# Seven-product projections at the border of layers 0 and 2, and PSUM rings kept by hand

## The chip, the core and the metric

The kernel runs on one core of one Trainium2 chip. The metric is the device time of one launch in microseconds (us), lower is better; three runs of the kernel before gave 2554.56 to 2558.83 us with a median of 2555.19 us.

## What is computed

Four images of 512 channels and 32 x 32 = 1024 positions (tokens), all in float32, pass through four residual layers. Cut to what matters:

```python
# layer 0: attention of 8 heads; scores mixed across heads, softmax, then an instance norm over each head's map
x = x + L0(_gn(x))
    q, k, v = w_q @ x, w_k @ x, w_v @ x            # 512x512 by 512x1024 each
    attn = softmax(einsum('gh,bhqT->bgqT', w_head, q k^T * scale))
    attn = (attn - mean) / sqrt(var + EPS) * in_gamma + in_beta
    out = (attn v).reshape(b, t, c) @ w_proj.T + b_proj
# layer 1: a gate per channel from the means of the channels
x = x + L1(_gn(x))
# layer 2: plain attention of 8 heads
x = x + L2(_gn(x))
    q = Wq @ x + bq;  k, v = split(Wkv @ x + bkv)
    out = Wp @ (softmax(q k^T * SCALE) v) + bp
# layer 3: 2048 memory rows of 512; the best 8 of each token, weighted by a softmax
x = x + L3(_gn(x))
```

`_gn` is a group norm of 32 groups. A projection is a 512 x 512 matrix by a 512 x 1024 image.

## The kernel before

All of the work that the change touches is in `fast_net`. Channels lie on 128 partitions with four blocks of them (`KC` = 4) along the free side; tokens are taken in two halves of 512 (`NB`). Images go through layer 0 one after the other, then through layer 2 one after the other, then tiles of 128 tokens through layer 3. Layer 1 is a vector of factors, found by a chain of small operations (`gating`, L861) and folded into the norm of layer 2.

**Layer 0.** An image has 32 steps of 32 query rows (`step`, L1436): scores, a relay of the scores through DMA queues to another layout (`scores`, `relays`), mixing of heads, exponentials, transposes, statistics, and seven steps later the product with v (`apply`). `STEPS` to `STEPS + LAG - 1` (32 to 38, loop at L1559) are tail steps: they finish the image's last seven `apply` calls, and the first four of them make q of the next image as `piece` (L1525). Every four steps a bank of PSUM (`pv_bank`) is full and `take_out` (L590) copies it away on ScalarE; in `step` this call stands after `piece` and the exponentials (L1482). `first` (L294) is the start of the launch: it loads image 0 and its weights, takes the norm's statistics block by block (`stats`, `means`, `deviations`, `normalize`), and multiplies each block as it is ready. Ahead of it the loads of nine small constants are written, on the ACT queue.

**The border.** After image 3's tail steps (`last`, L1563 to 1588) come k of layer 2's image 0 (`take_k2` through `project`, L186), the instance norm of image 3 (`instance_norm`, `norm_quarter`), v of image 0 (`take_v2` through `project_tokens`), and the output projection of image 3 (`put_out`, L729). Each is a plain projection: 4 output blocks x 4 input blocks x 2 halves = 32 products of 128 x 128 by 512 columns. q of image 0 is made in the tail steps and stays as it is in the change.

**Layer 2.** An image has 16 units (`UNITS2`, L945): 4 pairs of heads x 2 halves of queries x 2 halves of keys. `scores2` (L1165) makes four score tiles of a unit and their exponentials, and in between multiplies the unit before with v (`apply2`). Sums of the exponentials go through GpSimd and VectorE (`over_keys`), are inverted (`invert2`) and applied (`finish2`). Between two images there is a border again: q of the next image (`take_q2`, plain, evacuated on VectorE), the last `apply2`, then k, v and the output projection of the image before by seven products (`seven`, L1033).

**Seven products.** The two operands are cut into 2 x 2 blocks (256 x 256 of the weight, 256 x 512 of the image). Block sums and differences are made on VectorE (`weight_sums`, `input_sums`: five each, some in place), seven block products are made instead of eight, and their results are added up on VectorE; where a result block begins, ScalarE (or VectorE for v) writes it with the bias. A block product is 2 x 2 = 4 products of 128 x 128 by 512 columns, 28 in place of 32 in all. For images 1 and 2 the sums of the weights come back from DRAM (`w_sums`), those of image 1's weights are made once and stored.

**What sets the order.** TensorE, VectorE and ScalarE work in the order of the program (`pin` keeps it); a tile scheduler places the unpinned operations and the DMA issues. [...] In layer 0 six of them are three fixed pairs (`pairs`) and two are `pv_bank` and `pt_bank`; for layer 2 these are given back (`stage.close()`, L1590) and two pools take their place, `ps_s` with three pairs in turn, which also serves the small results (`small_ps`, L1597), and `ps_m` with two single banks.

The seven products and their uses, in order:

```python
    SEVEN = (
        (1, ((0, 0, "="), (1, 1, "="))),
        (4, ((0, 0, "+"), (1, 0, "="))),
        (3, ((0, 1, "="), (1, 1, "+"))),
        (5, ((0, 0, "-"), (0, 1, "+"))),
        (2, ((1, 0, "+"), (1, 1, "-"))),
        (7, ((0, 0, "+"),)),
        (6, ((1, 1, "+"),)),
    )
```

Of the kernel before, what the change touches and what calls it, by code (L numbers as in the profile page):

```python
# [10 lines left out]
F32 = mybir.dt.float32  # L11
# [5 lines left out]
P = 128  # L17
# [24 lines left out]
def fast_net(ctx: ExitStack, tc: tile.TileContext, a: dict, out: bass.AP, flag: bass.AP):  # L42
# [19 lines left out]


    def chan(src, name):
        t = const.tile([P, KC], F32, tag=name, name=name)
        nc.scalar.dma_start(out=t, in_=src)
        return t

    gamma = const.tile([P, NH], F32, tag="gamma", name="gamma")
    nc.scalar.dma_start(out=gamma, in_=a["in_gamma"].partition_broadcast(P))  # L70
    beta = const.tile([P, NH], F32, tag="beta", name="beta")
    nc.scalar.dma_start(out=beta, in_=a["in_beta"].partition_broadcast(P))
    bproj = chan(a["b_proj"], "bproj")
    bq2 = chan(a["bq"], "bq2")
    bk2 = chan(a["bk"], "bk2")
    bp2 = chan(a["bp"], "bp2")
    fcb = chan(a["fc_b"], "fcb")

    fcw = const.tile([NQ, C], F32, tag="fcw", name="fcw")
    nc.scalar.dma_start(out=fcw, in_=a["fc_w"])  # L80
    qpar = const.tile([P, NL * NQ], F32, tag="qpar", name="qpar")
    nc.scalar.dma_start(out=qpar, in_=a["q_params"].partition_broadcast(P))
# [3 lines left out]
    ident = const.tile([P, P], F32, tag="ident", name="ident")  # L86
    make_identity(nc, ident)
    ones = const.tile([P, P], F32, tag="ones", name="ones")
    nc.gpsimd.memset(ones, 1.0)
# [13 lines left out]
    )  # L103
    NS = 32
# [71 lines left out]
    def place(at, name):  # L176

        return pairs[at % 3] if at is not None else ps_s.tile([P, 2, NB], F32, tag="sc", name=name)
# [107 lines left out]

    def run_out(gen):
        for _ in gen:
            pass
# [4 lines left out]
    def first():  # L294
# [3 lines left out]
        w = I["w_q"] = eight_k([P, KC, C], "w_q0_0", 0)  # L298
        for k in range(KC):
            nc.sync.dma_start(out=xn[:, k, :], in_=x_v[0, :, k, :])  # L300
            nc.sync.dma_start(out=w[:, k, :], in_=a["w_q"][:, k, :])
        I["w_k"] = load_w("w_k", "w_k0_0", 1)
# [5 lines left out]
        def stats(k):  # L308
            mv = small.tile([P, 2], F32, tag="mv0", name=f"mv0_{k}")
            st = small.tile([P, 2, 6], F32, tag="bnst", name=f"st_a0_{k}")  # L310
            for i in range(2):
                pin(nc.vector.bn_stats(st[:, i, :], xn[:, k, i * NB:(i + 1) * NB]))
            pin(nc.vector.bn_aggr(mv, st.rearrange("p i s -> p (i s)")))
            parts[k] = group_coeffs_parts(mv[:, 0:1], mv[:, 1:2], f"a0_{k}")

        def means(k):
            next(parts[k])
            next(parts[k])

        def deviations(k):  # L320
            next(parts[k])
            found[k] = next(parts[k])
# [15 lines left out]
        stats(0)  # L338
        means(0)
        stats(1)  # L340
        deviations(0)
        means(1)
        normalize(0)
        for k in range(KC):
            if k + 2 < KC:
                stats(k + 2)
# [634 lines left out]
    def load2(b):  # L981
        for key in ("Wq", "Wk", "Wv"):
            load_sums(b, key, b == 1 or key == "Wq")

    def load_sums(b, key, plain):
        w = img[b][key] = eight_k([P, KC, C], f"{key}2_{b}")
        nc.sync.dma_start(out=w, in_=a[key] if plain else w_sums[key])

    H = C // 2
    w_sums = {key: dram.tile([P, KC, C], F32, tag=f"ws_{key}", name=f"ws_{key}")  # L990
              for key in ("Wk", "Wv", "Wp")}
# [15 lines left out]
    def weight_sums(b, key):  # L1007
# [4 lines left out]
        add7(s1, a11, a22)  # L1012
        sub7(s7, a12, a22)
        add7(a12, a11, a12)
        sub7(s6, a21, a11)
        add7(a21, a21, a22)
        nc.sync.dma_start(out=w_sums[key], in_=w)

# [14 lines left out]
    def seven(b, key, src, multiply, view, block, begin, done=None):  # L1033
# [3 lines left out]
        b11, t6, t7, b22 = quarters(src, NB)  # L1037
# [1395 lines left out]
```

## Time and profile before

| what | value |
| --- | --- |
| median of three runs | 2555.19 us |
| the profiled execution's own time | 2558.39 us |
| its span, first to last instruction | 2556.6 us |
| mean granted TensorE clock | 0.998 |
| PE (matmul) busy | 2503.3 us, 98% |
| PEld (weight load) busy | 1180.8 us, 46% |
| DVE (VectorE) busy | 1685.8 us, 66% |
| ACT (ScalarE) busy | 985.8 us, 39% |
| POOL (GpSimd) busy | 1192.5 us, 47% |

Each instruction of an engine is one row of the trace, with its start, its length, its line in the code, and `out<-in` by the names of the tiles. A float32 product shows as two PE rows, so a product of 512 columns is two rows of 0.43 us. "Idle before, releaser" is how long the engine stood still ahead of a row and which instruction ended that. `PE pair L192 x64` in the chain of work is 64 rows of line 192 that lay on the path to the end. In the strip of 40 slices a digit is the busy share in tenths.

### The profile page before, as it was taken

What the parts mean: (1) busy time and instruction counts of PE and PEld (TensorE: products, weight loads), DVE (VectorE), ACT (ScalarE), POOL (GpSimd) and SP (SyncE); (2) the same over time, 40 slices, a digit from 0 to 9 for tenths busy, and PEclk for the clock granted to TensorE, in tenths of its full rate; (3) what the DMA queues carried; (4) which work ended last, traced back from release to release, by engine and by line L of the source; (5) the groups of instructions that cost most, each with busy time, mean ns of one, the idle gap of its engine ahead of it and who ended that gap; (6) DMA issues with size and microseconds to landing.
All of it is one profiled execution on the core that took longest, in us unless ns stands there. A gap on an engine that the chain in (4) does not pass through costs nothing.

```text
span 2556.6 us, 47828 instructions
## 1 busy us (share of the span) xinstructions
PE 2503.3 (98%) x18534; PEld 1180.8 (46%) x18534; DVE 1685.8 (66%) x2785; ACT 985.8 (39%) x1177; POOL 1192.5 (47%) x1700
## 2 busy tenths in 40 slices
PE   8999999999999999999999999999999999999998
PEld 3344534554355534555633533453353344444445
DVE  4599448872688438881267567576657648788875
ACT  1467336651666336651153145125314612121211
POOL 3266415553465425553074147117405617566655
PEclk9999999999999999999999999999999999999999
DMA  2578438872698428982301130121014046767665
GB/s 83 145 207 237 125 120 226 244 211 74 172 243 235 131 82 211 244 248 101 124 16 55 70 112 18 54 83 59 21 54 148 18 130 190 219 186 217 187 184 170
DMA packets 187211, 361.39 MB, mean 141 GB/s; under 512 B 32729, under 2 KB 96217, under 8 KB 182882
## 3 DMA queue, kind: packets, MB, share of 16 engines
q1 hardware_dynamic: 105744, 178.71, 22.6%
q0 software_dynamic: 49152, 142.79, 20.6%
q10 hardware_dynamic: 32082, 36.76, 5.3%
q8 instruction: 149, 2.44, 0.4%
q14 instruction: 84, 0.69, 0.1%
HBM read 186.96 MB, written 36.96 MB: 88 GB/s over the span
## 4 chain that ended last, share of the span: by engine, by line
PE 74%; issue 10%; POOL 7%; DVE 3%; ACT 3%; DMA 2%; POOLq 0%; SPq 0%; ACTq 0%; DVEq 0%
PE pair L192 10%; PE sc_c L1183 9%; PE pv_c L1220 9%; PE pv L532 8%; POOL got L1360 7%; PE pair L467 6%; PE pair L493 5%; PE pt L425 5%; PE pt L721 4%; PE q L192 3%; PE Wk L1056 3%; PE Wv L1063 3%; ACT e L500 2%; PE Wp L1056 2%; PE at L1335 2%
## 5 line engine op out<-in xcount | busy, mean ns | idle before, releaser
L482 POOL DMA_DIRECT2D s<-ss x512 | 258.2, 511 | 399.5 <-PE pair L493 113.4
L506 DVE STREAM_TRANSPOSE eT<-e 128x1024 f32<-128x1024 f32 x256 | 316.5, 1236 | 193.6 <-ACT e L500 193.0
L1360 POOL DMA_INDIRECT got<-in_mem,ix x256 | 279.5, 1092 | 213.2 <-issue 122.1
L1177 ACT ACTIVATE eT<-sc_c 128x1024 f32<-128x1024 f32 x256 | 248.0, 1022 | 330.7 <-PE sc_c L1183 204.8
L521 DVE BATCH_NORM_STATS2 st<-e 128x6 f32<-128x256 f32 x1024 | 350.7, 404 | 0.0
L500 ACT ACTIVATE e<-pair 128x1024 f32<-128x1024 f32 x256 | 250.7, 1022 | 167.5 <-PE pair L493 137.2
L1201 POOL TENSOR_TENSOR e<-eT 128x1024 f32<-128x1024 f32 x96 | 232.3, 2421 | 168.6 <-DVE out L1125 69.5
L467 PE MATMUL pair<-k,q 64*32 64x512 f32 x4096 | 267.4, 598 | 12.7 <-ACT e L500 12.7
L473 ACT COPY ss<-pair 128x1024 f32<-128x1024 f32 x256 | 247.3, 1020 | 77.5 <-DMA s<-ss 37.9
L532 PE MATMUL pv<-eT,v 128*64 128x128 f32 x4096 | 250.7, 276 | 8.9 <-ACT pv L592 8.9
L532 PEld LDWEIGHTS pv<-eT,v 128*64 128x64 f32 x4096 | 221.1, 137 | 76.7 <-issue 54.5
L1183 PE MATMUL sc_c<-q,k 64*128 64x512 f32 x1024 | 240.9, 607 | 3.1 <-DVE xr L684 2.3
L1220 PE MATMUL pv_c<-eT,v 128*64 128x512 f32 x1024 | 233.0, 597 | 0.0
L1202 DVE TENSOR_TENSOR eT<-eT,e 128x1024 f32<-128x1024 f32 x96 | 136.3, 1420 | 146.3 <-POOL e L1201 146.1
L1197 POOL TENSOR_TENSOR eT<-eT 128x1024 f32<-128x1024 f32 x32 | 77.8, 2433 | 206.8 <-ACT eT L1177 202.8
L1407 DVE SCALAR_TENSOR_TENSOR acc<-got,et,acc 128x512 f32<-128x512 f32 x210 | 157.9, 752 | 7.5
L493 PE MATMUL pair<-s,wmix 32*32 32x512 f32 x4096 | 160.6, 600 | 2.3 <-issue 2.1
L1183 PEld LDWEIGHTS sc_c<-q,k 64*128 64x128 f32 x1024 | 93.6, 187 | 141.0 <-issue 71.9
L1340 ACT COPY att<-at 128x1024 f32<-128x1024 f32 (+1 forms) x65 | 64.9, 999 | 219.7 <-PE at L1335 212.9
L467 PEld LDWEIGHTS pair<-k,q 64*32 64x32 f32 x4096 | 57.0, 105 | 179.9 <-ACT e L500 86.2
L1220 PEld LDWEIGHTS pv_c<-eT,v 128*64 128x64 f32 x1024 | 68.0, 137 | 136.8 <-issue 136.8
L1335 PE MATMUL at<-memT,xn_d 128*128 128x512 f32 x256 | 120.7, 594 | 0.0
(335 smaller groups left out, 3431.3 us busy)
## 6 DMA issues: line engine op xcount, KB each, us to landing
s<-ss SPq DMA_DIRECT2D x512, 128.0 KB
s<-ss POOLq DMA_DIRECT2D x512, 128.0 KB
rb<-r POOLq DMA_DIRECT2D x64, 128.0 KB
o<-o SPq DMA_DIRECT2D x32, 256.0 KB
xr<-in_x ACTq DMA_DIRECT2D x32, 256.0 KB
x<-xr SPq DMA_DIRECT2D x32, 256.0 KB
xr_c<-x SPq DMA_DIRECT2D x32, 256.0 KB
rb_c<-r SPq DMA_DIRECT2D x64, 128.0 KB
```

Source lines behind the costliest of these rows:

```text
L192: pin(nc.tensor.matmul(ps[:, n, :], w[:, k, m * P:(m + 1) * P], rhs(k, n), start=(k == 0), stop=(k == KC - 1),))
L467: pin(nc.tensor.matmul(sc[m * NS:(m + 1) * NS, r, :], q[r * HD:(r + 1) * HD, m, s * NS:(s + 1) * NS], k_[r * HD:(r + 1) * HD, m, n * NB:(n ...
L482: pin(relays[side].dma_start(out=s2[2 * m + r::NH], in_=ss[m * NS:(m + 1) * NS, r, :]))
L493: pin(nc.tensor.matmul(mixed(s, r // 2)[t * NS:(t + 1) * NS, r % 2, :].rearrange("p (qq k) -> p qq k", qq=2), wmix[r * NS:(r + 1) * NS], s ...
L500: pin(nc.scalar.activation(e[:, half].rearrange("p r qq k -> p (r qq k)"), flat2(mixed(s, half)), AF.Exp))
L506: pin(nc.vector.transpose(eT[:, j % 2].rearrange("p b (qq i r) x -> p i r qq b x", qq=2, i=4)[:, i, 2 * half:2 * half + 2], e[:, half].rea ...
L521: pin(nc.vector.bn_stats(st[:, i, 2 * half + r, qq, :], e[:, half, r, qq, :]))
L532: pin(nc.tensor.matmul(pv[r * HD:(r + 1) * HD, gp, :], I["v"][:, t, g * HD:(g + 1) * HD], eT[:, j % 2, t, :, 4 * g:4 * g + 4], start=(t == ...
L1177: pin(nc.scalar.activation(e, scs[len(es)], AF.Exp))
L1183: pin(nc.tensor.matmul(sc[:, r, :], I["k"][r * HD:(r + 1) * HD, m, t * P:(t + 1) * P], I["q"][r * HD:(r + 1) * HD, m, n * NB:(n + 1) * NB] ...
L1220: pin(nc.tensor.matmul(pv[r * HD:(r + 1) * HD, :], I["v"][:, t, h * HD:(h + 1) * HD], e[:, r, :], start=(t == 0), stop=(t == TC - 1),))
L1360: pin(nc.gpsimd.indirect_dma_start(out=got[:, i, :], out_offset=None, in_=a["mem"], in_offset=bass.IndirectOffsetOnAxis(ap=ix[:, i:i + 1], ...
```

## The change

Six things change.

1. The start: the small constants' loads are written after the image's and the weights' loads, the first block of the image is loaded in halves, the means' arithmetic moves from GpSimd to VectorE, the statistics of block 1 are split around the deviations of block 0, and 17 products of a matrix of ones with itself are put on TensorE ahead of the first real ones.
2. `take_out` stands before `piece` in the tail steps.
3. At the border k, v and the output projection go by seven products. Their sums are spread: the input sums and the first weight sums over the tail steps 35 to 38, the others over the products. The output projection's inputs are strided pieces of 256 columns (`of_quarters`, `by_channels_of`), and `seven_collected` adds the residual, takes the statistics and stores.
4. q of layer 2's images 1 to 3 goes by seven products, with `Wq`'s sums made in image 0's units and kept in DRAM; `Wq` and `Wp` share the places of their other sums, so these three are loaded anew each time. The last `apply2` of an image moves ahead of q, and SCALE moves from q's evacuation into the exponential. Two of the input sums' three early adds move to the end of the units, one into unit 14.
5. `pairs`, `pv_bank` and `pt_bank` stay for layers 2 and 3; `next_pair` and `next_bank` take turns by hand. In the first unit after an output projection the third and fourth score tile leave out the pair that the last product is in (`late`).
6. At the borders of layer 2 the small results go to the idle one of the two single banks, not to a pair.

```diff
+    def next_pair(late=False):
+        if late:
+            ring[0:2] = ring[1::-1]
+        ring.append(ring.pop(0))
+        return pairs[ring[-1]]
...
+        for n in range(2):
+            nc.sync.dma_start(out=xn[:, 0, n * NB:(n + 1) * NB], in_=x_v[0, :, 0, n * NB:(n + 1) * NB])
         for k in range(KC):
-            nc.sync.dma_start(out=xn[:, k, :], in_=x_v[0, :, k, :])
+            if k > 0:
+                nc.sync.dma_start(out=xn[:, k, :], in_=x_v[0, :, k, :])
             nc.sync.dma_start(out=w[:, k, :], in_=a["w_q"][:, k, :])
+        for load in later:
+            load()
...
         def means(k):
-            next(parts[k])
-            next(parts[k])
+            mv = parts[k][0]
+            ps = small_ps(f"gps_a0_{k}")
+            pin(nc.tensor.matmul(ps[:, 0:1], gavg, mv[:, 0:1], start=True, stop=True))
+            dm, sq, gm = (column(name, k) for name in ("dm", "gsq", "gm"))
+            pin(nc.vector.tensor_sub(dm, mv[:, 0:1], ps[:, 0:1]))
+            pin(nc.vector.scalar_tensor_tensor(sq, dm, dm, mv[:, 1:2], ALU.mult, ALU.add))
+            pin(nc.vector.tensor_copy(gm, ps[:, 0:1]))
...
+        def warm(times):
+            for _ in range(times):
+                pin(nc.tensor.matmul(pairs[2][:, 0, 0:P], ones, ones, start=True, stop=True))
...
-        stats(0)
+        warm(11)
+        for i in range(2):
+            stats(0, i)
         means(0)
-        stats(1)
+        stats(1, 0)
+        warm(2)
         deviations(0)
+        stats(1, 1)
+        warm(2)
+        normalize(0)
         means(1)
-        normalize(0)
+        warm(2)
...
     def load_sums(b, key, plain):
         w = img[b][key] = eight_k([P, KC, C], f"{key}2_{b}")
         nc.sync.dma_start(out=w, in_=a[key] if plain else w_sums[key])
+        if not plain and key in w_more:
+            for i in range(3):
+                nc.sync.dma_start(out=places7[key][i], in_=w_more[key][:, i])
...
         for i, (at, uses) in enumerate(SEVEN):
-            ps = ps_s.tile([P, 2, NB], F32, tag="sc", name=f"{key}_{b}_{at}")
+            ps = next_pair()
             multiply(ps, *factors[at])
...
+    def by_channels_of(ps, w, x):
+        if not isinstance(x, list):
+            return by_channels(ps, w, x)
+        Q = NB // 2
+        for m in range(2):
+            for n in range(2):
+                for k in range(2):
+                    pin(nc.tensor.matmul(
+                        ps[:, m, n * Q:(n + 1) * Q], w[:, k, m * P:(m + 1) * P], x[2 * n + k],
+                        start=(k == 0), stop=(k == 1)))
...
+    def output_sums(b):
+        b11, b12, b21, b22 = of_quarters(b)
+        t1, t3, t4 = ([t[:, k, n * (NB // 2):(n + 1) * (NB // 2)].rearrange(
+            "p (g j x) -> p g j x", g=2, j=TC) for n in range(2) for k in range(2)]
+            for t in places7["in"])
+        for fn, out, x, y in (
+                (add7, t1, b11, b22), (sub7, t4, b21, b11), (sub7, t3, b12, b22),
+                (add7, b21, b21, b22), (add7, b12, b11, b12)):
+            yield [(lambda fn=fn, part=part: fn(*part)) for part in zip(out, x, y)]
...
+    def seven_collected(b):
...
+        def begin(i, j, ps):
+            for m in range(2 * i, 2 * i + 2):
+                pin(nc.scalar.activation(
+                    dst[:, m, j * NB:(j + 1) * NB], ps[:, m % 2, :],
+                    AF.Identity, bias=bproj[:, m:m + 1]))
+
+        def done(i, j):
+            for m in range(2 * i, 2 * i + 2):
+                part = dst[:, m, j * NB:(j + 1) * NB]
+                add7(part, part, rows.pop((m, j)))
+                pin(nc.vector.bn_stats(I["stb"][:, m, j, :], part))
...
-            pin(nc.scalar.activation(e, scs[len(es)], AF.Exp))
+            pin(nc.scalar.activation(e, scs[len(es)], AF.Exp, scale=SCALE))
...
-            sc = ps_s.tile([P, 2, NB], F32, tag="sc", name=f"sc_{nm}_{t}")
+            sc = next_pair(i >= 2 and u == UNITS2[b > 0])
...
         if tiled:
             apply(b, s - LAG)
+        if s >= STEPS and tiled and part == 3:
+            take_out(b, j)
         if not tiled or s >= STEPS:
             piece(b, s)
...
-        if tiled and part == 3:
+        if tiled and part == 3 and s < STEPS:
             take_out(b, j)
...
+            if last and s == STEPS + 3:
+                border_places()
+                first7, rest7 = input_sums(nxt["xn"])
+                of_k = weight_sums(0, "Wk", False)
+            if last and s >= STEPS + 3:
+                take7((first7 + (lambda: next(of_k),))[s - STEPS - 3])
+                if s == STEPS + 3:
+                    next(of_k)
...
+            for i, _ in enumerate(seven_by_channels(0, "k", bk2)):
+                next(state["behind"], None)
+                if i < 3:
+                    run_some(of_k, (1, 2, 1)[i])
+                if i in (1, 2):
+                    rest7[i - 1]()
+                if i >= 3:
+                    next(norm, None)
+                    run_some(of_v, (1, 2, 2, 1)[i - 3])
+                    run_some(of_p, (1, 0, 0, 1)[i - 3])
...
-            for i in range(TC // 2):
-                take_v2(0, i, i + 2)
-            for m in range(KC):
-                put_out(b, m, m)
-
-    stage.close()
-    pairs.clear()
+            sums7 = output_sums(b)
+            for i, _ in enumerate(seven_v(0)):
+                if i < 2:
+                    run_some(of_p, (2, 2)[i])
+                else:
+                    for fn in next(sums7):
+                        fn()
+            seven_collected(b)
...
     def small_ps(name):
-        return ps_s.tile([P, 2 * NB], F32, tag="sc", name=name)
+        return (pv_bank, pt_bank)[(turns[1] + 1) % 2] if at_border[0] else flat2(next_pair())
...
+            if s == 9 and b == 0:
+                weights = weight_sums(1, "Wq")
+            if s >= 10 and b == 0:
+                next(weights, None)
+            if s == len(UNITS2) - 2 and not last:
+                run_out(ahead)
+                first7, rest7 = input_sums(img[b + 1]["xn"])
+                first7[0]()
         run_out(ahead)
+        if not last:
+            first7[1]()
+            first7[2]()
+        apply2(b, UNITS2[-1])
...
-        for m in range(KC):
-            take_q2(b + 1, m)
-            if m < 3:
-                early[m]()
-            if b == 0 and m < 2:
-                weight_sums(1, ("Wk", "Wv")[m])
+        over_keys(b, *UNITS2[-1][:2])
+        at_border[0] = True
+        for i, _ in enumerate(seven_by_channels(b + 1, "q", bq2)):
+            if 1 <= i < 3:
+                rest7[i - 1]()
+            if i == 4:
+                invert2(b)
+            if i == 5 and b == 0:
+                run_out(weight_sums(1, "Wk"))
             next(behind, None)
         load_sums(b, "Wp", b == 0)
-        apply2(b, UNITS2[-1])
```

## The prediction

> **What bounds the kernel now.** I read the page's busy shares first.
>
> ```profile
> span 2556.6 us, 47828 instructions
> ...
> PE 2503.3 (98%) x18534; PEld 1180.8 (46%) x18534; DVE 1685.8 (66%) x2785; ACT 985.8 (39%) x1177; POOL 1192.5 (47%) x1700
> ```
>
> TensorE stands still for 53.3 us in all. So a gain is TensorE rows taken out, or a piece of those 53 us, and a cost is a new wait of TensorE. Next, what ended its waits (total, times, longest, in us):
>
> ```profile
> PE pv L532 <- ACT pv L592: 8.9, 15, 1.6
> PE pt L145 <- DVE mv L313: 7.3, 1, 7.3
> ...
> PE sc_c L1183 <- DVE xr L684: 2.3, 1, 2.3
> PE Wk L1056 <- ACT k L1073: 2.0, 1, 2.0
> ...
> PE pt L891 <- POOL amp L883: 0.6, 1, 0.6
> ```
>
> The change touches what stands behind each of these. (The largest, 12.7 us of L467 behind ACT in layer 0's steps, it leaves alone.) Then the timeline of TensorE, a plain projection and its neighbour at the border, and the seven products of v at a border of layer 2 (start, length, rows at the end):
>
> ```profile
> 1209.83 27.71 PE L204 MATMUL pair<-Wv_n,xn_all 128*128 128x512 f32 x64
> 1237.38 27.79 PE L745 MATMUL pair<-eT 128*128 128x256 f32 x128
> ...
> 1662.35 3.62 PE L1063 MATMUL Wv<-eT,sums 128*128 128x256 f32 x16
> 1665.81 7.07 PE L1063 MATMUL Wv<-Wv,sums 128*128 128x256 f32 x32
> 1672.71 7.07 PE L1063 MATMUL Wv<-Wv,xn_c 128*128 128x256 f32 x32
> 1679.62 7.07 PE L1063 MATMUL Wv<-eT,xn_c 128*128 128x256 f32 x32
> 1686.62 3.70 PE L1183 MATMUL sc_c<-q,k 64*128 64x512 f32 x16
> ```
>
> A plain projection is 64 rows of 512 columns in 27.7 us, 0.433 us each. Seven products take 1662.35 to 1686.62 = 24.3 us, 3.47 us a product, with no wait among them although VectorE adds every result. Rows of 256 columns (L745) take 0.216 us, so the strided halves lose nothing. Last, VectorE's groups at the first border of layer 2 (busy, mean ns, idle before):
>
> ```profile
> L993 DVE TENSOR_TENSOR k<-k,Wk 128x1024 f32<-128x1024 f32 x8 | 9.6, 1218 | 5.4 <-PE Wk L1056 3.1 <-ACT k L1073 2.3
> L1202 DVE TENSOR_TENSOR eT<-eT,e 128x1024 f32<-128x1024 f32 x6 | 9.4, 1566 | 9.4 <-POOL e L1201 9.4
> L993 DVE TENSOR_TENSOR eT<-Wk 128x512 f32<-128x512 f32 x3 | 2.0, 684 | 0.0
> ```
>
> [...]L1202 above, beside GpSimd's adds, has a mean of 1.57 us against 1.22 for the same shape elsewhere[...]. At the start the first four rows of L332 take 3.78 us (0.95 each)[...].
>
> **The change part by part.** Against the profiled execution, 2558.39 us (span 2556.6).
>
> *Products at the border.* k, v and the output projection of image 3: 27.7 - 24.3 = 3.4 each, 10.2 us less. Does VectorE keep up with 3.47 us a product? k: eight adds of 1.16 (1.22 less the overlap of neighbours) = 9.3, ten weight sums of 0.65 = 6.5, two input sums 2.3: 18.1 of 24.3. v: twelve of 1.16 = 13.9, three weight sums 2.0, twenty strided adds of 0.4 = 8: 23.9, nearly as much as TensorE. Placed in order, VectorE ends v 3.3 us behind TensorE; a pair comes back after three products, 10.4 us, so TensorE doesn't see it. The output projection: eight adds 9.3, residual adds 8 x 0.65, statistics 8 x 0.69, 20.8 with the rest. It is the shape of layer 2's output projection, which also runs unbroken. The output sums need the instance norm: its product stands before k's last product, then about 3.5 us on GpSimd (1210.26 to 1213.5 before) and 5.8 us on ScalarE, done some 5 us before the third product of v is out. ScalarE's writes, 8 x 0.69 a projection, have room (ScalarE is nearly idle there).
>
> *What the tail steps get.* Step 35 puts an input sum (1.22) and a weight sum (0.68) on VectorE right behind the q of that step. What is queued behind them is seen here:
>
> ```profile
> 1172.28 1.28 DVE L1145 TENSOR_SCALAR q<-pair,bq 128x1024 f32<-128x1024 f32 x1 [7.73 <-PE pair L192]
> 1173.48 0.35 DVE L559 RECIPROCAL ri<-pt 128x32 f32<-128x32 f32 x1
> 1173.87 0.42 DVE L561 SCALAR_TENSOR_TENSOR seen<-ri,seen 128x32 f32<-128x32 f32 x2
> 1174.63 0.16 DVE L130 COPY amp<-pt 128x4 f32<-128x4 f32 x1 [0.35 <-PE pt L886]
> ```
>
> The inverse ri and the copy of amp come 1.9 us later. GpSimd's queue starts with the store of ri, then `scale`, then the gate's rotations, and L891, already 0.6 us late, waits for these: 1.9 us more. TensorE's next row is k's first product, so nothing covers it. From both sides: 0 if GpSimd finds slack, 3 if the second pair of sums delays the copy as well. I take 1.9.
>
> *The first scores after the border.* L1183 waited 2.3 us for the last evacuations. With the last product's pair left out the first four score tiles need pairs that are free or that an exponential (1.02 us) frees. I place eight tiles at 8.8 us after the last product; before it was 1276.31 - 1265.18 = 11.1: 2.3 us less (0 to 2.3).
>
> *`take_out`.* In images 0, 1 and 2, step 34 copies q (1.01 us) on ScalarE before pv, and L532 waits 1.59, 1.47 and 1.47 us for pv. With pv first, its 0.59 us lies under the 7 us of q's product: 4.5 us less. Image 3 had q on VectorE and no such wait.
>
> *q of layer 2.* Three times 27.7 - 24.3 = 10.2 us less. VectorE has 8 x 1.16 in place of 4 x 1.28, and 2.3 of input sums. The last `apply2`, now ahead of q, needs exponentials that end two microseconds before it. The tightest is the second input sum: it stands behind an add that waits for GpSimd, and is done 1.8 us before the second product wants it: 0, or up to 1 each[...]. Image 0's Wk, Wv and Wp sums (3.3 us each) fall where 3.47 us a product leaves 2.3 idle, with two pairs in hand. The new loads and stores (256 KB each) wait on SP for products that end before the next inverse is due, except Wp's load, which stands ahead of ri's store until q is done; rb then comes about 5.5 us into k, and the next k add is due at 6.9. I cost these at nothing; without that cover it is 1 to 2 us a border.
>
> *Small results in the idle bank.* The 2.0 us of L1056 behind ACT k occur once, where gate and inverse took pairs between two products: 2.0 us less.
>
> *Scores after layer 2's output projections.* Sixteen rows take 4.69 us there against 3.70 elsewhere, hidden waits of 1 us. By my placing 0.3 comes back each time: 0.9 (0 to 3).
>
> *The start.* Products of ones run while TensorE waits (7.3 us), so they cost nothing and should spare up to 1.9 us of half rate. But w_q's second block was issued only at 8.32, behind the wait for bproj's load (6.1 us on SP), and block 2 landed at 13.78. Statistics of block 2 stand on VectorE ahead of block 1's normalizing, so block 1's products can't start before that landing plus 3.2 us. With less in front, it may land 1 us sooner, or 2; the new order also puts a wait for the second load on the first. Between -3.3 (the full chain) and +0.5. I take -1.0.
>
> Sum: -10.2 + 1.9 - 2.3 - 4.5 - 10.2 - 2.0 - 0.9 - 1.0 = -29.2, so 2529.2 for that execution. It stood 3.2 us above the median of 2555.19, which gives 2526.0.
>
> **The rivals.** *VectorE becomes the bound at the borders.* For it: v's 23.9 us in 24.3[...]. Against: GpSimd is busy 9.4 us of the 86 us from 1182 to 1268. Strided adds at the 512 price (0.69) give 5.4 us more, of which TensorE sees 2; a norm that ends 8 us later makes it wait 3; 2 us at each q for the second sum. In all 11 us: 2537. *The clock gives way (the slower one).* The table by stage shows a granted clock of 0.93 at 1268 to 1290, against 1.00 around it. If fewer bubbles made such stretches longer all over the kernel, each 0.01 of mean clock would cost about 25 us; from 0.986 down the gain of 29 is gone, and 0.98 gives 2571. Against: PE is busy 98% already at 0.998, and the change adds only 0.5% to that.
>
> **How the numbers follow.** The forecast 0.82, from 2520 to 2533 (all open terms at their good ends: 2519). VectorE 0.13, 2533 to 2545. The clock 0.03, and 0.02 for a mix that ends within 0.2% (5.1 us, about what a measurement of this kernel can tell from no change). Faster 0.95, same 0.02, slower 0.03. The range 2520 to 2537 leaves out half of the VectorE case, the clock, and a little of the first.
>
> **What would show it.** 28 in place of 32 products at six projections, 24.3 us each and no gap; no wait of L532 for pv near 1.5 us; no wait of the first scores on the residual; a wait of about 2.5 us before the gate's second product. Wrong: gaps among v's or the collected products ended by VectorE, a second q product that waits for its sum, a mean clock under 0.99.

## The result, and the profile after

The changed kernel takes 2541.64 us (median of six runs, 2533.77 to 2544.57) against 2555.98 us of the kernel before beside it: ratio 0.9938, 95% interval 0.9925 to 0.9952. It is faster, as forecast, but by 14.3 us (0.6%) and not by 29: the time lies above the forecast's range of 2520 to 2537. The profiled execution took 2542.59 us. First the busy shares:

```profile
span 2540.9 us, 47980 instructions
...
PE 2492.0 (98%) x18544; PEld 1182.5 (47%) x18544; DVE 1764.4 (69%) x2874; ACT 1006.5 (40%) x1213; POOL 1210.7 (48%) x1688
```

VectorE got 89 operations more. PE is busy 11.3 us less, though six times 3.4 = 20 us of products were taken out: some of what is left, or was added, runs longer. What ended TensorE's waits (total, times, longest):

```profile
PE pt L152 <- DVE eT L1412: 5.1, 2, 2.6
PE pv L575 <- ACT pv L635: 4.3, 12, 1.0
...
PE pt L934 <- POOL amp L926: 2.5, 1, 2.5
PE pair L1386 <- DVE s_c L1372: 2.0, 1, 2.0
...
PE pt L929 <- DVE ri L602: 1.4, 1, 1.4
PE pt L1355 <- DVE eT L1412: 1.1, 1, 1.1
PE pair L1318 <- DVE sum L1041: 0.9, 1, 0.9
PE pair L1109 <- DVE sums L1041: 0.7, 1, 0.7
```

The wait for pv fell from 8.9 to 4.3, and those of L1183 and L1056 are gone. But L152, L934, L929, L1386 and L1355 together wait 12 us; of these, the list of before has only the gate's 0.6. The timeline of TensorE at layer 0's border (start, length, rows; in brackets the idle time before and its releaser):

```profile
1170.21 0.35 PE L929 MATMUL pt<-amp,turn 128*128 128x4 f32 x2 [1.43 <-DVE ri L602]
...
1176.72 0.38 PE L934 MATMUL pt<-amp,turn 128*128 128x2 f32 x2 [2.52 <-POOL amp L926]
...
1177.19 5.38 PE L1109 MATMUL pair<-eT 128*128 128x512 f32 x8
1182.40 3.60 PE L1109 MATMUL pair<-eT,Wk_n 128*128 128x512 f32 x8
...
1205.08 3.62 PE L1198 MATMUL pair<-eT 128*128 128x256 f32 x16
1208.53 7.07 PE L1198 MATMUL pair<-Wv_n,eT 128*128 128x256 f32 x32
...
1229.25 10.46 PE L1109 MATMUL pair<-eT 128*128 128x512 f32 x24
1239.55 13.98 PE L1120 MATMUL pair<-eT 128*128 128x256 f32 x64
1253.46 2.08 PE L1318 MATMUL pair<-q,k 64*128 64x512 f32 x8
```

v runs unbroken from 1205.08 to 1229.25, 24.17 us, and the output projection to 1253.46, 24.21. These are the forecast's 24.3. But k's first product, behind two waits of the gate, takes 5.38 us for eight rows where the next takes 3.60. The same at the second border of layer 2:

```profile
1594.80 3.70 PE L1109 MATMUL pair<-sums,eT 128*128 128x512 f32 x8
1601.15 0.59 PE L152 MATMUL pt<-mv_d,gavg 128*128 128x4 f32 x2 [2.65 <-DVE eT L1412]
1601.60 10.04 PE L1109 MATMUL pair<-sums,Wq 128*128 128x512 f32 x16
1611.48 0.28 PE L162 MATMUL pt<-gsq_d,gavg 128*128 128x4 f32 x2
```

Sixteen rows that need 7.0 take 10.04 behind a wait of 2.65. The table by stage says why (stretch, its length, busy us of PE, PEld, DVE, ACT, POOL, then PEclk; the last two columns are the DMA's):

```profile
1601.50:1603.00 1.50, 1.50 (x4) 0.92 (x4) 1.50 (x4) 0.16 (x1) 0.60 (x3) 0.50 0.00 0
1603.00:1605.00 2.00, 2.00 (x3) 0.67 (x2) 0.47 (x1) 0.00 (x0) 0.00 (x0) 0.50 0.49 150
...
1609.00:1611.00 2.00, 2.00 (x6) 0.86 (x5) 1.67 (x2) 1.27 (x2) 0.00 (x0) 1.00 0.00 0
```

TensorE was granted half its clock after the wait (0.50), and the full clock again by 1609 (1.00). PE counts as busy there, so no list of waits shows this loss. What L152 waited for is on VectorE's timeline:

```profile
1596.69 2.35 DVE L1041 TENSOR_TENSOR sums<-xn_c 128x1024 f32<-128x1024 f32 x2
1600.41 0.69 DVE L1412 TENSOR_TENSOR eT<-pt,rb_c 128x512 f32<-128x512 f32 x1 [1.36 <-DMA rb_c<-r]
```

L152 writes to the "idle" bank `pt`. That bank still holds the pv of the half of the queries before the last until `finish2` multiplies it by rb (L1412). L1412 stands behind two sums in VectorE's queue, but these were done 1.36 us before it: what it waited for last is the load of rb. At the same border before the change, TensorE and VectorE (L1277 is this multiplication there):

```profile
1606.08 7.13 PE L192 MATMUL q<-xn_c,Wq 128*128 128x512 f32 x16
```

```profile
1612.57 0.68 DVE L1277 TENSOR_TENSOR eT<-pv_c,rb_c 128x512 f32<-128x512 f32 x1
```

Counted from the start of q, the multiplication ended 7.2 us in before the change and ends 6.3 us in after it (1601.10 against 1594.80). So it isn't late at this border by its own measure. What is new is who needs its bank: a small product that stands behind the first of q's products, 3.7 us in.

The groups of VectorE from k to the output projection at the first border of layer 2, to compare with the two L993 lines of before:

```profile
L1041 DVE TENSOR_TENSOR k<-k,pair 128x1024 f32<-128x1024 f32 x8 | 9.4, 1209 | 8.3 <-PE pair L1109 4.8 <-ACT zr L135 3.4
...
L1041 DVE TENSOR_TENSOR eT<-Wv 128x512 f32<-128x512 f32 x3 | 2.0, 684 | 0.0
```

1209 and 684 ns, and VectorE waits for TensorE: in the seven products themselves it isn't the bound.

Where the change of the time lies, from milestones in the timelines of TensorE (lengths of stages; the last column is the kernel with both mends, shown below):

| stage | before | forecast | after | both mends |
| --- | --- | --- | --- | --- |
| start to k's first product | 1179.3 | -3.6 | -2.1 | -2.7 |
| to the last inverse product of image 0's units (L1251, L1386) | 199.3 | -12.5 | -10.5 | -12.2 |
| to the first scores behind that border | 116.7 | -5.7 | -4.5 | -4.8 |
| image 1's units, same ends | 107.0 | 0 | +2.4 | +2.4 |
| their border | 112.1 | -3.7 | +2.3 | -3.8 |
| image 2's units | 107.0 | 0 | 0 | 0 |
| their border | 112.1 | -3.7 | +0.6 | -3.8 |
| to the last product with the memory (L1335, L1470) | 595.4 | 0 | 0 | 0 |
| sum | | -29.2 | -11.8 | -24.9 |

Behind the last of these products lies the end, the last gathered rows and stores. It took 27.6 us in the profiled execution of before and 23.8 in that of after; over the profiled runs of changed kernels below it took 23.4 to 24.8 (eight) or 27.3 to 27.6 (three), the same kernel once 24.0 and once 27.3. So those 3.8 us of the profiles' difference are not put down to the change, and no stage of the table has them.

### The profile page after: what moved, and what is told of

Same layout as the page of the kernel before. It is cut to its first block, busy times and chain, and to the rows that moved or that the text cites. A ratio compares the mean times of both kernels' runs of the same rounds, so it can differ in the third digit from the quotient of the medians.

```text
span 2540.9 us, 47980 instructions
## 1 busy us (share of the span) xinstructions
PE 2492.0 (98%) x18544; PEld 1182.5 (47%) x18544; DVE 1764.4 (69%) x2874; ACT 1006.5 (40%) x1213; POOL 1210.7 (48%) x1688
## 4 chain that ended last, share of the span: by engine, by line
PE 69%; issue 10%; POOL 8%; DVE 6%; DMA 4%; ACT 2%; SPq 0%; POOLq 0%; ACTq 0%; DVEq 0%
PE pair L199 10%; PE pair L1109 9%; PE pv L575 8%; PE pair L1318 8%; POOL got L1495 7%; PE pair L510 6%; PE pair L536 5%; PE pt L468 5%; PE pair L1198 4%; PE pt L1355 4%; PE pt L764 4%; PE pv L1355 3%; ACT e L543 2%; DMA s<-ss 2%; PE pair L1470 2%
## 5 line engine op out<-in xcount | busy, mean ns | idle before, releaser
L1312 ACT ACTIVATE eT<-pair 128x1024 f32<-128x1024 f32 x256 | 248.3, 1022 | 320.1 <-PE pair L1318 197.9
L1336 POOL TENSOR_TENSOR e<-eT 128x1024 f32<-128x1024 f32 x96 | 240.2, 2506 | 168.6 <-ACT eT L1312 118.2
L510 PE MATMUL pair<-k,q 64*32 64x512 f32 x4096 | 267.3, 598 | 12.8 <-ACT e L543 12.8
L1318 PE MATMUL pair<-q,k 64*128 64x512 f32 x1024 | 239.9, 605 | 2.1 <-DVE sum L1041 0.9
L1337 DVE TENSOR_TENSOR eT<-eT,e 128x1024 f32<-128x1024 f32 x96 | 148.3, 1545 | 125.2 <-POOL e L1336 125.0
L1332 POOL TENSOR_TENSOR eT<-eT 128x1024 f32<-128x1024 f32 x32 | 84.1, 2628 | 201.7 <-ACT eT L1312 195.7
L536 PE MATMUL pair<-s,wmix 32*32 32x512 f32 x4096 | 159.9, 600 | 2.8 <-DMA s<-ss 2.6
L1318 PEld LDWEIGHTS pair<-q,k 64*128 64x128 f32 x1024 | 92.3, 186 | 140.4 <-issue 66.6
L1475 ACT COPY att<-pair 128x1024 f32<-128x1024 f32 (+1 forms) x65 | 64.9, 999 | 220.2 <-PE pair L1470 199.8
L510 PEld LDWEIGHTS pair<-k,q 64*32 64x32 f32 x4096 | 57.0, 105 | 179.9 <-ACT e L543 86.5
L1490 DVE MAX8 top<-att 128x8 f32<-128x2048 f32 x31 | 71.1, 2293 | 73.1 <-ACT att L1475 38.5
L1470 PE MATMUL pair<-memT,xn_d 128*128 128x512 f32 x256 | 120.7, 594 | 0.0
L1470 PE MATMUL pair<-memT,eT 128*128 128x512 f32 x256 | 120.4, 593 | 0.0
```

What stands on the lines that cost most here:

```text
L510: pin(nc.tensor.matmul(sc[m * NS:(m + 1) * NS, r, :], q[r * HD:(r + 1) * HD, m, s * NS:(s + 1) * NS], k_[r * HD:(r + 1) * HD, m, n * NB:(n ...
L536: pin(nc.tensor.matmul(mixed(s, r // 2)[t * NS:(t + 1) * NS, r % 2, :].rearrange("p (qq k) -> p qq k", qq=2), wmix[r * NS:(r + 1) * NS], s ...
L1312: pin(nc.scalar.activation(e, scs[len(es)], AF.Exp, scale=SCALE))
L1318: pin(nc.tensor.matmul(sc[:, r, :], I["k"][r * HD:(r + 1) * HD, m, t * P:(t + 1) * P], I["q"][r * HD:(r + 1) * HD, m, n * NB:(n + 1) * NB] ...
L1470: pin(nc.tensor.matmul(sc[:, i0 - lo:i0 - lo + NB], xn3[b][:, k, tt * P:(tt + 1) * P], memT[k][:, i0:i0 + NB], start=(k == 0), stop=(k == ...
```

## The experiments

**Theory A.** The missing gain went into new waits of TensorE, L152's above all (2.65 and 2.46 us) and the gate's (1.43 and 2.52, 0.62 before), and such a wait of about 2.5 us is followed by half the clock, which costs nearly as much again (10.04 us for sixteen rows that need 7.0). **B:** VectorE is the bound, and the waits only show it. **C:** the half rate is a throttle by load that comes whether TensorE waited or not. The first four kernels ran on one chip with 2555.44 us before, the next four with 2557.46, the last three with 2556.33. Both mends, measured twice, gave 2526.23 and 2530.36; so where two kernels were measured at different times and lie less than some 4 us apart, the profiles decide below, not the medians.

**Late small results.**

```diff
-            next(behind, None)
+            if b == 0 or i in (2, 3, 5, 6):
+                next(behind, None)
         load_sums(b, "Wp", b == 0)
```

> Everything of the change stays; only at layer 2's borders of images 1 and 2 the small products of the third norm (L152, L162 of the changed kernel) move from behind q's first and third product to behind its third and sixth, so that the idle bank's last reader (L1412) is done before. Theory A (the missing gain went into new waits of TensorE, and each wait of about 2.5 us is followed by some 5 us at half TensorE clock): the two waits (2.65 and 2.46 us) go, and with them the half-rate products behind (3.1 and 1.9 us too long): 10 us less than the changed kernel's 2541.6, so 2531.5. Theory B (VectorE bounds the border, the bank's wait only shows that it is late): the time goes to the next product, 2540 to 2542. Theory C (the half rate is a throttle that comes whether TensorE waited or not): only the waits go, 2536.5.

Measured: 2529.92 us, ratio 0.9901 [0.9886, 0.9916]. The timeline of TensorE at the same border:

```profile
1589.74 3.70 PE L1109 MATMUL pair<-sums,eT 128*128 128x512 f32 x8
1593.27 7.03 PE L1109 MATMUL pair<-sums,Wq 128*128 128x512 f32 x16
1600.14 0.28 PE L152 MATMUL pt<-mv_d,gavg 128*128 128x4 f32 x2
1600.28 7.11 PE L1109 MATMUL pair<-xn_c,Wq 128*128 128x512 f32 x16
```

No wait, and 7.03 us in place of 10.04. B falls for these two borders, as VectorE's work is the same and in the same order; that the half rate went with the waits speaks against C. The 11.7 us between the medians are 1.7 more than these waits and their half rate. In the profiled execution two more things were absent that this edit doesn't touch: L1386's wait of 2.0, and the half rate at k's first product (3.68 us), although the gate's wait before it was there with 2.50.

**Early sums.**

```diff
+    def tail_sums(s):
+        if s == STEPS + 3:
+            for fn in first7 + (lambda: next(of_k), lambda: next(of_k)):
+                fn()
...
-                 lambda b, s: qs[s - STEPS](s + 1) if s < STEPS + KC else None)
...
-            if last and s >= STEPS + 3:
-                take7((first7 + (lambda: next(of_k),))[s - STEPS - 3])
-                if s == STEPS + 3:
-                    next(of_k)
+                 lambda b, s: (last and tail_sums(s), qs[s - STEPS](s + 1))
+                 if s < STEPS + KC else None)
```

> Only the four early sums of layer 0's border (three of the image, the first two of k's weights: t1, t4, t3, s1, s7) move: from behind q's last evacuation in the tail steps 35 to 38 to ahead of it on VectorE, into the 7.7 us in which VectorE waits for q's product. Theory A: the waits of the gate's two small products (1.43 and 2.52 us, 0.62 before the change) go back to about 0.6, and k's first product, no longer behind a long wait, takes 3.6 us and not 5.4: 5 us less than 2541.6, so 2536.5. Theory B (these sums have no slack anywhere, or GpSimd's own chain is what is late): within 1 us of 2541.6. Theory C: the waits only, 2538.3.

Measured: 2538.03 us, ratio 0.9928 [0.9915, 0.9942]; 3.6 less than the changed kernel. TensorE's timeline:

```profile
1174.34 0.38 PE L934 MATMUL pt<-amp,turn 128*128 128x2 f32 x2 [0.63 <-POOL amp L926]
...
1174.81 3.68 PE L1109 MATMUL pair<-eT 128*128 128x512 f32 x8
```

The wait is back at 0.63, and L929 has none. k's first product is at 3.68; since it took 3.68 behind a wait of 2.50 in the run with late small results too, this run shows the waits to be the sums' doing, but not the half rate. How the sums had made the gate late is seen on VectorE (q's last evacuation) and on GpSimd, first in the changed kernel, then here:

```profile
1166.78 1.28 DVE L1280 TENSOR_SCALAR q<-pair,bq 128x1024 f32<-128x1024 f32 x1 [7.73 <-PE pair L199]
...
1170.68 3.03 DVE L1041 TENSOR_TENSOR eT<-xn_all 128x1024 f32<-128x1024 f32 x2
```

```profile
1171.03 3.42 POOL L648 TENSOR_TENSOR o<-pv,rb 64x256 f32<-64x256 f32 x2
```

```profile
1167.75 1.28 DVE L1280 TENSOR_SCALAR q<-pair,bq 128x1024 f32<-128x1024 f32 x1 [1.80 <-PE pair L199]
```

```profile
1170.27 1.81 POOL L648 TENSOR_TENSOR o<-pv,rb 64x256 f32<-64x256 f32 x2
```

The scaling ahead of the gate's rotations (L648) starts 4.25 us behind the start of q's evacuation in the changed kernel and 2.52 here, 1.7 us through VectorE's queue. And it took 1.6 us longer in the changed kernel, where two sums of VectorE (L1041) lay beside it. Both rows were longer there than apart: 3.42 us against 1.81 for L648, and 3.03 for the two sums against 2.34 for two adds of the same shape at 1219.25. So the sums cost their place in VectorE's queue and 1.6 us of GpSimd's time; together these are the 3.3 us by which the gate's two waits grew.

**The wait filled.** The wait for the bank is left as it is; TensorE is given work in it.

```diff
+            if b > 0 and i == 0:
+                for _ in range(11):
+                    pin(nc.tensor.matmul(
+                        pairs[ring[0]][:, 0, 0:P], ones, ones, start=True, stop=True))
             next(behind, None)
```

> The wait for the idle bank stays at the borders of images 1 and 2, but TensorE fills it: 11 products of a matrix of ones with itself (128 columns, about 2.5 us in all) go into the pair that q's second product takes next, ahead of the small product that waits. Their results are overwritten. Theory A: the end of the wait stays where it is, TensorE keeps its clock, and the 3.1 and 1.9 us of half-rate products go: 2536.6. Theory B: no change, 2541.6. Theory C (a throttle by load): the same half rate, or more of it: 2541.6 or above.

Measured: 2539.74 us, ratio 0.9942 [0.9928, 0.9956]: 1.9 less than the changed kernel, less than the run-to-run spread of either (2537.74 to 2543.1 here), so the median doesn't decide. The timeline and the table by stage of its profiled execution do:

```profile
1593.97 3.70 PE L1109 MATMUL pair<-sums,eT 128*128 128x512 f32 x8
1597.51 2.62 PE L1840 MATMUL pair<-ones 128*128 128x128 f32 x22
1600.13 0.39 PE L152 MATMUL pt<-mv_d,gavg 128*128 128x4 f32 x2
1600.38 7.11 PE L1109 MATMUL pair<-sums,Wq 128*128 128x512 f32 x16
```

```profile
1597.50:1600.10 2.60, 2.60 (x23) 2.42 (x21) 1.42 (x3) 2.39 (x4) 0.00 (x0) 1.00 0.24 80
1600.40:1602.40 2.00, 2.00 (x7) 1.01 (x7) 2.00 (x4) 0.16 (x1) 0.60 (x3) 1.00 0.00 0
```

L152 starts as late after the first product as before (6.16 us behind 1593.97, 6.35 behind 1594.80), but at full clock, and the next products take 7.11 and not 10.04; at the other border 7.11 and not 8.78. Rows stayed fast behind some waits of this length (2.50 and 2.53 us, see the last section), so this execution alone wouldn't prove it. But in the five profiles of the last section the clock is halved in the middle of the kernel five times, each time behind a wait of 2.16 to 2.65 us. In these runs the half rate goes with the idleness, not with the load: C falls.

**Both mends.** The first two edits together.

> The late small products at layer 2's borders and the early sums at layer 0's border together. Theory A: both gains add, 15 us less than 2541.6, so 2526.5, which is what was predicted for the change. Theory B: within 2 us of 2541.6. Theory C: 2533.

Measured: 2526.23 us, ratio 0.9883 [0.9868, 0.9898]. Once more, beside the plain q below:

> The kernel with both mends once more, as the base for the two runs beside it on the same chip: 2526.2, 29 us under the kernel before, by theory A.

Measured: 2530.36 us, ratio 0.9886 [0.9864, 0.9908]. Against the kernel before beside them 29.2 and 26.0 us: by the medians the two mends give back nearly all that was missing.

**Single parts.** `take_out` put back behind `piece`:

```diff
-        if s >= STEPS and tiled and part == 3:
-            take_out(b, j)
...
-        if tiled and part == 3 and s < STEPS:
+        if tiled and part == 3:
             take_out(b, j)
```

> The changed kernel with the copy of pv in the tail steps put back behind q's piece and the exponentials, as it was before the change; nothing else. Theory A (this part did what was forecast): three waits of about 1.5 us for pv come back, 4.4 us more than 2541.6, so 2546. Rival (what it gained is hidden by the relay waits of the next steps anyway): 2541 to 2543.

Measured: 2546.77 us, ratio 0.9951 [0.9936, 0.9967], 5.1 more than the changed kernel. Its waits have the line of before again, so the 4.5 us of this step are shown:

```profile
PE pv L575 <- ACT pv L635: 8.9, 15, 1.6
```

The small results in pairs again:

```diff
-        return (pv_bank, pt_bank)[(turns[1] + 1) % 2] if at_border[0] else flat2(next_pair())
+        return flat2(next_pair())
```

> The changed kernel with the small results of the borders written to the next of the three pairs in turn, as before the change, and not to the idle single bank; nothing else, in particular they stay at their places in the order. Theory A: the waits for L1412 (2.65 and 2.46 us) and the half rate behind them (3.1 and 1.9 us) go, and waits of up to 2 us for a pair between two products come back in their place: 2531.5 to 2534. Theory B (VectorE is late at these borders whatever bank is used): 2540 to 2542. Should the part be worth the 2 us of the forecast: 2543.6.

Measured: 2533.83 us, ratio 0.9899 [0.9884, 0.9915], 7.8 less than the changed kernel. L152 no longer waits, and what comes in its place is this line of the waits, 1.0 us in three:

```profile
PE pair L1109 <- ACT q L1208: 1.0, 3, 0.6
```

So in the profiled executions this part of the change took about 1 us of waits away and put 10 in, waits and half rate together.

**The price of q's sums.** In the stretch of image 1's units the changed kernel has L1386's wait of 1.99 us. There the residual's third piece is loaded ahead:

```diff
-                tag, bufs = (("xr", 2), (("o1", "xs")[r], 1))[at % 2]
+                tag, bufs = (("xr", 2), (("o1", "xs")[r], 1), ("rb", 2), ("xr", 2))[at]
...
-            at = order.index((i, j)) + 2
+            at = order.index((i, j)) + 3
...
-        load(0)
-        load(1)
+        for at in range(3):
+            load(at)
```

> On top of the kernel with both mends (2526.2): in the output projection of layer 2 the residual's third piece is loaded at its beginning, into two buffers that are free there, and the fourth two products earlier. Theory: the one wait of L1386 in image 1's third unit (1.99 us for a sum that VectorE makes late) comes from that piece, which landed 1.1 us late behind the other loads of the SP queue and pushed VectorE's work into GpSimd's adds: the wait goes, 2524.2. Rival[...]: 2526.

Measured: 2524.66 us, ratio 0.9866 [0.985, 0.9883], the lowest median, though not clear of the 2526.23 of both mends. L1386 has no line among its waits, and image 1's units take 107.0 us as before the change, against 109.4. The run with late small results has no such wait either, without this edit: there VectorE stood 0.56 us for the load of that piece, with both mends 1.14. So the wait goes with the load's lateness, which differs between executions; seven of the eight profiles that have seven products for q and not this edit show the wait.

q by the plain projection, with `take_q2` for m = 0 to 3, `invert2` and image 0's sums of W_k behind m = 2, k's `rest7` behind k's second and third product, the small results behind m = 1 to 3 (0 to 3 in image 0). The loads, and what is left out:

```diff
-            load_sums(b, key, b == 1)
+            load_sums(b, key, b == 1 or key == "Wq")
...
-            if s == 9 and b == 0:
-                weights = weight_sums(1, "Wq")
-            if s >= 10 and b == 0:
-                next(weights, None)
...
-        for i, _ in enumerate(seven_by_channels(b + 1, "q", bq2)):
```

> On top of the kernel with both mends (2526.2): layer 2's q of images 1 to 3 goes by the plain projection again, with W_q loaded plain, and its sums are left out of image 0's units; k, v and the output stay as they are. If seven products for q are worth three times 3.4 us and nothing else hangs on them: 10.2 us more, 2536.4. If the waits that the changed kernel has in the units of images 0 and 1 (1.07 us for L1412 behind the weight sums, 1.99 us of L1386 behind the loads of the sums) are the price of q's sums: 10.2 less 3 to 4, so 2532.5 to 2533.5. If q by seven products had no net worth: 2526.

Measured: 2536.99 us, ratio 0.9921 [0.9907, 0.9935], 10.8 above the kernel with both mends, which had run on another chip. Beside it on one chip:

> The plain q of layer 2 once more, beside its base on the same chip. The first time the medians (taken on two chips) stood 10.8 us apart and the two profiled executions only some 5.6 after the start. If q's sums cost nothing in the units, the distance to the base is 10.2 us; if the waits of 1.05, 0.47 and 0.70 us in image 0's part and of 1.99 us in image 1's, which the profile of the plain q lacks, count in full, it is 10.2 - 4.2 = 6 us.

Measured: 2535.69 us, ratio 0.9910 [0.9892, 0.9927], 5.3 above its base. In the profiled executions the way from k's first product at layer 0's border to the end of image 2's border is 5.6 us longer than in the base in the first pair of profiles (737.8 against 732.2) and 5.5 in the second (738.2 against 732.7). The waits of L1386 for s_c and of q for its second sum have no line in its profile, and that of L1355 on bank `pt` has none either. So q's seven products are worth 5.5 us: the 10.2 that was forecast, less 4.7, of which these waits, with one of 0.45 for L1412 on bank `pv`, are 4.2 in the second base's profile. The remaining 0.5 stays open. The two distances of the medians, 10.8 and 5.3, show how much medians taken at two times, on two chips, can mislead.

**W_q's sums elsewhere.**

```diff
-            if s == 9 and b == 0:
+            if s == 7 and b == 0:
                 weights = weight_sums(1, "Wq")
-            if s >= 10 and b == 0:
-                next(weights, None)
+            if s in (7, 9, 11, 13) and b == 0:
+                run_some(weights, 1 + (s == 13))
+            if s == 14 and b == 0:
+                run_out(weights)
```

> On top of the kernel with both mends and the residual loaded ahead: W_q's five sums in image 0 stand behind units 7, 9, 11 and 13 (two there), in which no multiplication of a finished pv follows, and not behind units 9 to 14. Theory: the waits of L1355 for L1412 (1.05 and 0.47 us) come from the sum that stands ahead of L1412 on VectorE, and go: 1.5 us less, and with the residual 3.5 less than the kernel with both mends beside it, so 2522.7. Rival (L1412 is late by the inverse that it waits for[...]): 2524.2, only the residual's 2 us.

Measured: 2526.6 us, ratio 0.9876 [0.9854, 0.9897]: 3.8 under its base, but no gain over the kernel with the residual ahead (2524.66, measured at another time) is seen. The wait of 0.47 is gone, but so it is in one of the two profiles of both mends, so this isn't shown to be the edit's doing. That of 1.06 is still there:

```profile
1346.42 1.53 DVE L1018 TENSOR_SCALAR xn_c<-xn_c,sa,ta 128x1024 f32<-128x1024 f32 x2
1347.87 0.69 DVE L1041 TENSOR_TENSOR Wq<-Wq 128x512 f32<-128x512 f32 x1
1348.47 0.68 DVE L1412 TENSOR_TENSOR eT<-pt,rb_c 128x512 f32<-128x512 f32 x1
```

By the whole timeline VectorE works from 1332.19 to past 1349 there without a pause. A sum put a unit earlier slides along with the queue and still stands ahead of L1412. Whether earlier units would take it wasn't tried.

## Why the prediction was wrong

It named the sign, most stages and even the places of trouble; one step was wrong in kind, one too small, and one factor was missing. That the time lies in the span given to the first rival (2533 to 2545) is chance: the waits that made it are mostly others.

*The step that failed* is "Small results in the idle bank": "2.0 us less", with no cost. The bank isn't idle: it holds pv until `finish2`, which waits for the load of rb and ends 6.3 us behind the start of q, while the small product is due 3.7 us behind it. I had asked what the results no longer wait for (a pair), not what they wait for now. By the first experiment it cost about 10 us (5.1 of waits, 4.8 of half rate), by the one with the pairs it saved 1.

*The tail sums' term was too small.* "I take 1.9", with 3 as the bad end. The wait of 2.5 us ahead of the gate's second product came as forecast (2.52), but 1.43 came ahead of its first as well, and the two grew by 3.3: 1.7 through the queue, close to the 1.9, and 1.6 through GpSimd, whose scaling took 3.42 us beside the sums and 1.81 without them. I had allowed for longer rows of VectorE beside GpSimd's (1.57 us against 1.22), and not for a longer row of GpSimd in that chain. And the 7.7 us in which VectorE stood still ahead of q's evacuation, shown among the prediction's own lines, was the cover: the second experiment put all five sums in there, and no new wait of TensorE came of it.

*The missing factor* is the clock. A wait was priced at its own length. The second rival had the clock give way as a mean all over the kernel, below 0.99; the mean was 0.996, and the loss is local, behind waits: +1.8 us at k, +3.0 and +1.8 at the two borders, 6.6 in all in the profiled execution. It differs from one execution to the next: of the six, five with a mean clock of 0.996 or 0.997 took 2540.6 to 2544.6 us, and the one with 0.999 took 2533.77. The profile of before had it in sight: 0.93 at 1268 to 1290, which I quoted, follows the 2.32 us wait of L1183.

*q of layer 2* was costed too well: the products give 10.2, but the sums and loads "at nothing" cost 4.2 in waits (0.70 for the second sum, as the range of "up to 1 each" had it; 1.5 for L1412; 2.0 for L1386), of which the residual loaded ahead gets 2 back. The first rival, VectorE as the bound, is right in image 0's last units, at q's second sum, at the first scores behind layer 0's border (0.9) and, behind a late load, in image 1's first units; of the seven products none but that one of q waits for it.

*Right:* v and the output projection (24.17 and 24.21 against 24.3) with no gap by VectorE; k too but for its first product; `take_out` (4.6 of 4.5); the first scores (2.2 of 2.3). The start came 0.6 us sooner in the profiled execution against 1.0, but this isn't settled: in the other profiles of the changed start layer 0's first long wait (1.5 us in each, at L467 of before and L510) ends from 1.8 us sooner to 2.1 us later than in that of before. The spared "half rate" of "up to 1.9 us" there was an estimate from before's rows (3.78 us for the first four, 1.96 for the next four); after, the first four of L368 took 3.15 us, with a granted clock of 0.52 at 10 to 12 us, and the next four 1.96. The 0.4 us of a strided add was the author's estimate too; the twenty took 0.416 us each in the profile of after. Of 17.4 us that the stages miss, 13.1 came back with both mends. The medians, 14.3 less than before, stand 2.5 better than the stages; what lies at the end varies by more than that.

## What to carry over

A buffer is idle when its last reader is done, not when its next writer is far: before a result is moved to another bank, find that reader, its place in its engine's queue, and what it waits for itself. Price a wait of a busy TensorE as long as those here (2.16 to 2.65 us) with a range: its length, and on top of it nothing, as behind two of 2.50 and 2.53 us, or the 1.8 to 3.0 us of half rate of the changed kernel. Look for that part in the granted clock, since no list of waits has it. Sums for fewer products belong where their engine stands still already, and away from rows of GpSimd that lie on a chain (3.42 us beside two sums, 1.81 without).

## What the runs showed of the hardware

Half the clock behind so short a pause was in no term of the forecast. In five profiles (before; after; both mends and plain q, each the second time; W_q's sums elsewhere) the granted clock falls to 0.50 between 30 and 2500 us behind five pauses of TensorE: 2.32 us in before (ahead of L1183), 2.52, 2.65 and 2.46 us in after (ahead of L934 and, twice, of L152), and 2.16 us with the plain q (ahead of L536; a mean of 0.66 from 720 to 725). It stayed whole there behind all shorter pauses, up to the 1.99 us of L1386 in after and with both mends. Half the clock lasted 3.41 us in before and at two places in after, and 6.83 us behind after's pause of 2.65; what this cost was 1.8 to 3.0 us at after's three pauses. Before 30 us the changed kernel has 3.41 us of it behind a pause of 1.60 us.

The rows didn't slow down behind every pause of some 2.5 us. In the run with late small results eight rows of k took 3.68 us behind one of 2.50 us; in the run with `take_out` put back sixteen rows took 7.11 us behind one of 2.53 us:

```profile
1827.17 0.39 PE L152 MATMUL pt<-mv_d,gavg 128*128 128x4 f32 x2 [2.53 <-DVE eT L1412]
1827.41 7.11 PE L1109 MATMUL pair<-sums,Wq 128*128 128x512 f32 x16
```

So length alone doesn't decide; what else does was not shown. With products of ones in the pause, 2.6 us of them, the clock read 1.00 at the one border that was tabled, and the sixteen rows behind took 7.11 us at both.
